# Self-attention with outputs of three of four key tiles moved to the following slot

## Chip, cores and metric

The kernel runs on one core of a Trainium2 chip. The metric is the device time of one execution in microseconds (us). Engines are named as the profile names them: PE is TensorE's matmul, PEld its weight load, DVE is VectorE, ACT is ScalarE, POOL is GpSimd, SP is SyncE. Each engine works through its own list of instructions in order, and waits for the others by semaphores.

## The reference

The input `x` is 8 batches of 512 rows of width 512 in float32. It passes through a cross-attention block with adaptive layer norm, and then through a diffusion transformer block: self-attention, cross-attention to a context of 77 rows per batch, and an MLP. Only self-attention bears on the change:

```python
x_norm = modulate(_ln(x), shift_a, scale_a)
qkv = x_norm @ W_qkv + b_qkv
q, k, v = jnp.split(qkv, 3, axis=-1)          # 16 heads of 32
...
attn_w = jax.nn.softmax(jnp.einsum('bhqd,bhkd->bhqk', q, k) * scale, axis=-1)
attn_out = jnp.einsum('bhqk,bhkd->bhqd', attn_w, v)
...
attn_out = attn_out @ W_proj + b_proj
x = x + gate_a[:, None] * attn_out
```

## The kernel before

The program has four phases, one after the other: cross-attention "x", self-attention "a", cross-attention "c", and the MLP. Self-attention is the function `self_phase`. In it the order of all instructions is the order of the Python statements, on every engine; nothing is rescheduled.

The work is cut into 32 groups: batch `b` (0 to 7) times `fc` (0 to 3), where one `fc` is four heads, 128 columns. A group has 512 keys, cut into four key tiles `k` of 128, and all 512 queries. Scores are held transposed, keys on the partitions and queries along the row. Two heads share a tile of 128 x 1024, so each key tile has two tiles `e`. The steps of a group, as methods of `Group`:

- `scores(k)`: eight matmuls (`sT_a`, L803) write two PSUM tiles. ACT copies each to `e` (L821); from k = 1 on DVE takes a running maximum over the key tiles into `mx_a` (L823). Both PSUM tiles of the pool are used by one score step, so the next one needs the copies and maxima done.
- `maxima()`: DVE transposes and reduces `mx_a` (L834, L835) to `part_a`, four times.
- `spread()`: PE transposes `part_a` (`mxT_ps_a`, L843), DVE reduces it and negates it (L847), SP writes it to DRAM as `mxd_a` (L852).
- `shift(k)`: POOL issues two DMAs (L857) that read `mxd_a`, the same row for all 128 partitions, and add it to the two `e` tiles of 512 KB. Per group that is eight DMAs, 4.19 MB.
- `exp(k)`: ACT, in place, two instructions (L866).
- `add_up(k)`: adds the two `e` tiles to the sum over key tiles, on POOL for k = 1 and 2, on DVE for k = 3 (L873).
- `outputs(k)`: eight matmuls (L886) accumulate `o_ps_a` over the key tiles.
- `total()`: eight matmuls with ones (L896) give the denominators `z_ps_a`.
- `finish()`: DVE takes the reciprocal (L903) and multiplies (L906) into `oT_a`.

The main loop has 31 passes; a pass is called a slot here. In a slot, group `g` is shifted, exponentiated and summed with V, while the scores of the next group `nxt` are made. In between stand TensorE's other tasks of the slot, given by `beside(b, fc)` as four pieces f[0] to f[3] of eight matmuls each: values, queries and keys of later groups, and the output projections of the batch before (`project`, L353, with the residual sum on DVE at L772, products and sums on POOL at L775 and L776 in `flush(0)`, stores on SP at L779 in `flush(1)`). In fc 2, `transpose_x` adds four groups of PE transposes (L724), and `load_x` loads the next batch's rows. In fc 0, `load_tile` loads four residual tiles `xr_a` (L718). `normalise_x` feeds layer norm pieces to DVE.

The `e` tiles come from two pools of eight, one for even and one for odd groups: group n + 1 takes the tiles of group n - 1. PSUM has four banks for scores, two for the pool `ps_m` that projections, values, queries, keys and transposes share, and two for `o_ps_a` and `z_ps_a`.

Of the kernel before, what the change touches and what calls it, by code (L numbers as in the profile page):

```python
# [10 lines left out]
F32 = mybir.dt.float32  # L11
# [7 lines left out]
P = 128  # L19
H = 512  # L20
# [59 lines left out]
def tile_pixart_block(ctx: ExitStack, tc: tile.TileContext, a: dict, out: bass.AP):  # L80
    nc = tc.nc
    x, ctx_in, cond = a["x"], a["ctx_1024"], a["cond_1024"]
    B, N, _ = x.shape
    S = ctx_in.shape[1]
    NT = N // P
# [272 lines left out]
    def run(gen):  # L358
        while True:
            try:  # L360
                next(gen)
            except StopIteration as stop:
                return stop.value
# [28 lines left out]
    def normalise_x(nm, b):  # L392

        xb = [x_sb[nm, 0][:, t, :] for t in range(NT)]
        mv, y = yield from ln_stats_pieces(xb, P, 1e-6, f"{nm}{b}")
        yield
        for t in range(NT):
            normalise(xb[t], xb[t], mv, y, t, P)
            if t % 2:
                yield  # L400


    with tc.tile_pool(name="ps_s", bufs=2, space=PSUM, reuse_waits="tile") as ps_s:
# [287 lines left out]
        def self_phase(w, bo_row, work, work_2, ctx_c):  # L691
# [14 lines left out]
            def flush(part):  # L706

                while later[part]:
                    later[part].popleft()()

            def load_x(b):
                nc.scalar.dma_start(
                    out=x_cur, in_=x_src["a"][b].rearrange("(t p) d -> p t d", p=P)
                )

            def load_tile(b, t, queue=nc.scalar):
                xr = work.tile([P, H], F32, tag="xr", bufs=4, name=f"xr_a{b}_{t}")
                queue.dma_start(out=xr, in_=x_src["a"][b][ts(t, P), :])  # L718
                st[b]["x"][t] = xr

            def transpose_x(b, k):
                pt = ps_m.tile([P, H], F32, tag="m", name=f"lnT_ps_a{b}_{k}")
                for t in range(NT):
                    nc.tensor.transpose(pt[:, ts(t, P)], x_cur[:, t, ts(k, P)], ident)  # L724
                o = work.tile([P, N], F32, tag="xnT", bufs=5, name=f"xnT_a{b}_{k}")
                nc.scalar.activation(  # L726
                    o, pt, AF.Identity,
                    bias=mod_l1[:, k, b : b + 1], scale=mod_l1[:, KC + k, b : b + 1],
                )
                st[b]["xT"].append(o)  # L730
# [54 lines left out]
            class Group:  # L785
# [91 lines left out]
                def outputs(self, k):  # L877

                    if k == 0:
                        self.po, self.pz = [  # L880
                            ps_o.tile([P, H], F32, tag="o", name=f"{nm}_ps_{self.nm}")
                            for nm in "oz"
                        ]
                    vt = st[self.b]["v"][k]
                    for h in range(4):
                        nc.tensor.matmul(  # L886
                            self.po[ts(h, HD), :],
                            lhsT=vt[:, self.fc * P + h * HD : self.fc * P + (h + 1) * HD],
                            rhs=self.e[k][h // 2][:, h % 2, :],
                            start=(k == 0), stop=(k == NT - 1),  # L890
                        )

                def total(self):

                    for h in range(4):
                        nc.tensor.matmul(  # L896
                            self.pz[ts(h, HD), :], lhsT=ones, rhs=self.sum[:, h, :],
                            start=True, stop=True,
                        )
# [28 lines left out]
            def pump(gen, n):  # L928
                for _ in range(n):
                    next(gen, None)  # L930
# [10 lines left out]
                first.scores(k)  # L941
                run(gen)
            first.maxima()
            first.spread()
            last, ln = None, normalise_x("a", 1)
            for n, g in enumerate(groups[:-1]):
                b, fc = g.b, g.fc
                nxt = groups[n + 1]
                more = b + 1 < B
                f = beside(b, fc)  # L950
                if fc == 3:
                    ln = normalise_x("a", b + 2) if b + 2 < B else iter(())
                if fc == 0 and b > 0:
                    for t in range(NT):
                        load_tile(b - 1, t)
                for k in range(NT):
                    g.shift(k)
                flush(0)
                flush(1)
                if not more and fc == 1:  # L960
                    ctx_c.w_k = load_w("L1_xcond_W_kvc", 0)
                nxt.scores(0)
                if last is not None:
                    last.total()
                    last.finish()
                pump(f[0], 4)
                if fc == 2 and more:
                    transpose_x(b + 1, 0)
                    transpose_x(b + 1, 1)
                nxt.scores(1)  # L970
                if fc != 2 and more or fc == 2 and not more:
                    next(ln, None)
                g.exp(0)
                pump(f[1], 4)
                if fc == 1 and not more:
                    ctx_c.load()
                    ln = ctx_c.norm()
                if fc == 2 and more:
                    transpose_x(b + 1, 2)
                    transpose_x(b + 1, 3)  # L980
                nxt.scores(2)
                if fc == 1 and more:
                    for _ in ln:
                        pass
                elif fc != 2 and more or fc == 2 and not more:
                    next(ln, None)
                g.exp(1)
                flush(0)
                g.add_up(1)
                pump(f[2], 3)  # L990
                nxt.scores(3)
                pump(f[2], 1)
                g.exp(2)
                g.add_up(2)
                g.outputs(0)
                g.outputs(1)
                nxt.maxima()
                pump(f[3], 4)
                g.outputs(2)
                nxt.spread()  # L1000
                if fc == 2 and not more:
                    next(ln, None)
                g.exp(3)
                g.add_up(3)
                if fc == 2 and not more:
                    for _ in ln:
                        pass
                if fc == 2 and b + 2 < B:
                    load_x(b + 2)
                g.outputs(3)  # L1010
                last = g

            g = groups[-1]
            for k in range(NT):
                g.shift(k)
            flush(0)
            flush(1)
            work_2.release()
            kv = tc.alloc_tile_pool(name="kv_c", bufs=1, side="right", reuse_waits="tile")
            ctx_c.room(kv)  # L1020
            last.total()
            last.finish()
            ctx_c.transpose()
            run(ctx_c.values(0))
            run(ctx_c.values(1))
            value = None
            for k in range(NT):
# [348 lines left out]
```

## Time and profile before

| | us |
|---|---|
| three runs | 2659.38, 2662.30, 2663.26; median 2662.3 |
| the profiled execution: its time | 2658.09 |
| the profiled execution: its span | 2656.3 |
| PE busy in the span | 2519.7 (95%) |
| DVE / ACT / POOL busy in the span | 1742.3 / 1062.3 / 830.2 |
| mean granted TensorE clock | 0.984 |
| self-attention's slots (first to last issue of `mxd_a`) | 527.66 to 1398.36 |

The profile is of one execution. A row of a timeline gives the start, the duration, the engine, the line, the operation and its tiles, and in brackets how long the engine had been idle and who released it. Busy time of PE says little here, as the ends of matmuls are modelled; distances between starts say more. Rows of POOL with DMA_DIRECT2D are the issue of a DMA; when its data has landed is given separately.

### The profile page before, as it was taken

Reading aid. Unit: us, or ns where it says so; the run is one execution under the profiler, and the core shown is the slowest. Engines: PE = TensorE matmul, PEld = TensorE weight load, DVE = VectorE, ACT = ScalarE, POOL = GpSimd, SP = SyncE. Lnnn points to the kernel's source line nnn. Section 1 sums busy time; section 2 is a strip of 40 time slices with the busy share of each in tenths; the row PEclk is TensorE's granted clock in tenths of the full one; section 3 lists DMA queues with packets and bytes.
Section 4 is the critical chain, followed back from the end, with each engine's and each line's share of the span. In section 5 each row is a group of like instructions: output and inputs, shape, how many; then the busy total and the mean of one; then the engine's idle time right before and its main releaser. Section 6 shows DMA issues by size and latency. Waiting matters only on the chain.

```text
span 2656.3 us, 32748 instructions
## 1 busy us (share of the span) xinstructions
PE 2519.7 (95%) x12517; PEld 1436.6 (54%) x12517; DVE 1742.3 (66%) x3131; ACT 1062.3 (40%) x1442; POOL 830.2 (31%) x692
## 2 busy tenths in 40 slices
PE   7999999889999999999988999999999999999998
PEld 3555554322323333332323555555788888888887
DVE  2676677377777777877674777776655555555553
ACT  1533333366666676665663443442211211211220
POOL 1000001156766767677574010112211011011011
PEclk9999999999999999999998999999999999999999
DMA  7011211189898898998898111114011111111010
GB/s 261 28 52 52 80 57 68 64 162 185 174 179 181 176 194 178 179 185 174 174 195 225 60 40 53 40 42 137 16 37 38 30 36 38 30 36 40 28 36 24
DMA packets 116407, 264.90 MB, mean 100 GB/s; under 512 B 12594, under 2 KB 29058, under 8 KB 116250
## 3 DMA queue, kind: packets, MB, share of 16 engines
q0 software_dynamic: 37152, 134.28, 26.9%
q1 hardware_dynamic: 69125, 109.42, 12.4%
q10 hardware_dynamic: 9973, 19.11, 2.2%
q8 instruction: 99, 1.62, 0.2%
q14 instruction: 58, 0.48, 0.1%
HBM read 226.39 MB, written 36.37 MB: 99 GB/s over the span
## 4 chain that ended last, share of the span: by engine, by line
PE 40%; issue 26%; DMA 15%; DVE 9%; POOL 6%; ACT 4%; POOLq 0%; SPq 0%; ACTq 0%; DVEq 0%
DMA e_a<-mxd_a 12%; PE proj_ps_c L353 4%; PE proj_ps_x L353 4%; PE q_ps_c L345 4%; PE q_ps_x L345 4%; PE proj_ps_a L353 3%; PE sT_a L803 2%; PE pT_ps_c L621 2%; PE pT_ps_x L621 2%; DVE tu_a L834 2%; DVE part_a L835 2%; POOL res_m L1285 2%; POOL xr L1286 2%; DVE mx_a L823 2%; PE v_ps L353 2%
## 5 line engine op out<-in xcount | busy, mean ns | idle before, releaser
L821 ACT COPY e_a<-sT_a 128x1024 f32<-128x1024 f32 x256 | 253.5, 1012 | 155.0 <-PE sT_a L803 112.5
L866 ACT ACTIVATE e_a<-e_a 128x1024 f32<-128x1024 f32 x256 | 263.1, 1056 | 60.0 <-DMA e_a<-mxd_a 59.6
L857 POOL DMA_DIRECT2D e_a<-mxd_a x256 | 228.1, 2061 | 132.2 <-DMA mxd_a<-mxT_a 114.1
L1285 POOL TENSOR_TENSOR res_m<-res_m,gate_m 128x256 f32<-128x256 f32 x64 | 52.1, 814 | 665.9 <-DVE res_m L1283 665.9
L823 DVE TENSOR_TENSOR mx_a<-sT_a,mx_a 128x1024 f32<-128x1024 f32 x128 | 154.1, 1220 | 85.4 <-PE sT_a L803 59.7
L873 POOL TENSOR_TENSOR sum_a<-e_a,e_a 128x1024 f32<-128x1024 f32 x64 | 151.1, 2381 | 168.2 <-ACT e_a L866 168.2
L1219 ACT ACTIVATE hT<-hT,bcol 128x512 f32<-128x512 f32 x128 | 91.9, 721 | 237.4 <-DVE hT L1194 229.3
L886 PE MATMUL o_ps_a<-e_a,v 128*32 128x512 f32 x1024 | 167.8, 622 | 17.7 <-ACT e_a L866 17.4
L803 PE MATMUL sT_a<-qT_a,kT_a 32*128 32x512 f32 x1024 | 156.4, 666 | 20.2 <-ACT e_a L821 19.4
L372 POOL TENSOR_TENSOR x_x<-x_x,res_x 128x512 f32<-128x512 f32 x32 | 40.6, 1269 | 413.7 <-DVE res_x L368 255.2
L873 POOL TENSOR_TENSOR sum_a<-sum_a,e_a 128x1024 f32<-128x1024 f32 x64 | 149.9, 2364 | 9.0 <-ACT e_a L866 8.9
L622 ACT COPY pT_x<-pT_ps_x 77x512 f32<-77x512 f32 x128 | 72.9, 578 | 191.3 <-PE pT_ps_x L621 191.2
L903 DVE RECIPROCAL rz_a<-z_ps_a 128x512 f32<-128x512 f32 x32 | 107.4, 3357 | 63.9 <-PE z_ps_a L896 63.9
L372 POOL TENSOR_TENSOR x_c<-x_c,res_c 128x512 f32<-128x512 f32 x32 | 40.6, 1270 | 344.3 <-DVE res_c L368 287.5
L622 ACT COPY pT_c<-pT_ps_c 77x512 f32<-77x512 f32 x128 | 72.8, 577 | 162.8 <-PE pT_ps_c L621 162.8
L345 PE MATMUL q_ps_x<-xnT_x,w_L_xcond_Wq 128*128 128x512 f32 x256 | 135.1, 614 | 0.0
L1186 PE MATMUL q_ps_h<-x_m,w_L_xcond_W_mlp 128*128 128x256 f32 x512 | 132.3, 381 | 0.0
L345 PE MATMUL q_ps_a<-xnT_a,w_L_xcond_W_qkv 128*128 128x512 f32 x256 | 130.9, 637 | 0.7 <-ACT xnT_a L726 0.7
L1186 PE MATMUL q_ps_h<-xT_m,w_L_xcond_W_mlp 128*128 128x256 f32 x512 | 131.4, 379 | 0.0
L345 PE MATMUL q_ps_c<-xnT_c,w_L_xcond_W_qc 128*128 128x512 f32 x256 | 130.1, 594 | 0.0
L1186 PE MATMUL q_ps_h<-x_m,w_s 128*128 128x256 f32 x512 | 122.2, 382 | 5.9 <-DVE w_s L1140 4.9
L353 PE MATMUL v_ps<-w_L_xcond_W_qkv,xnT_a 128*128 128x512 f32 x256 | 118.9, 607 | 0.0
(248 smaller groups left out, 5016.0 us busy)
## 6 DMA issues: line engine op xcount, KB each, us to landing
e_a<-mxd_a POOLq DMA_DIRECT2D x256, 512.0 KB, 13.9
xa<-x_x SPq DMA_DIRECT2D x32, 256.0 KB, 2.0
xc<-xr_a SPq DMA_DIRECT2D x32, 256.0 KB, 2.6
x_c<-xc SPq DMA_DIRECT2D x8, 1024.0 KB, 6.3
w_L_xcond_W_mlp<-in_L_xcond_W_mlp_dram SPq DMA_DIRECT2D x8, 1024.0 KB, 6.1
xm<-x_c SPq DMA_DIRECT2D x32, 256.0 KB, 2.0
x_m<-xm SPq DMA_DIRECT2D x8, 1024.0 KB, 5.2
xr<-xm SPq DMA_DIRECT2D x64, 128.0 KB, 3.6
```

The costliest lines, as they stand in the source:

```text
L345: nc.tensor.matmul(ps, lhsT=w[:, k, ts(j, P)], rhs=xT[k], start=(k == 0), stop=(k == KC - 1))
L353: nc.tensor.matmul(ps, lhsT=xT[k][:, cols], rhs=w[:, k, :], start=(k == 0), stop=(k == KC - 1))
L622: nc.scalar.copy(pTs[-1][:, h % 2, :], pp[:S, :])
L803: nc.tensor.matmul(sc[h // 2][:, h % 2, :], lhsT=kT[ts(h, HD), ts(k, P)], rhs=qT[ts(h, HD), :], start=True, stop=True,)
L821: nc.scalar.copy(self.e[k][i], sc[i])
L823: nc.vector.tensor_tensor(self.mx[1 - i], sc[1 - i], self.e[0][1 - i] if k == 1 else self.mx[1 - i], ALU.max,)
L857: nc.gpsimd.dma_start(out=self.e[k][i].rearrange("p h n -> p (h n)"), in_=self.mxd[2 * i : 2 * i + 2, :] .rearrange("h n -> (h n)").partit ...
L866: nc.scalar.activation(self.e[k][i], self.e[k][i], AF.Exp)
L873: engine.tensor_tensor(sum_i, self.e[0][i] if k == 1 else sum_i, self.e[k][i], ALU.add)
L886: nc.tensor.matmul(self.po[ts(h, HD), :], lhsT=vt[:, self.fc * P + h * HD : self.fc * P + (h + 1) * HD], rhs=self.e[k][h // 2][:, h % 2, : ...
L903: nc.vector.reciprocal(r, self.pz)
L1186: nc.tensor.matmul(self.banks[n][:, half], lhsT=lhsT, rhs=rhs, start=(k == 0), stop=(k == len(pairs) - 1),)
```

## The change

The loop is rearranged; no arithmetic is added or taken away.

- Outputs of key tiles 1, 2 and 3 of group `g`, its `add_up(2)`, `add_up(3)`, `exp(3)`, `total` and `finish` move to the slot after. There they stand behind the score step of `nxt` that precedes the one taking that tile's buffers: outputs 1 after scores 0, outputs 2 after scores 1, outputs 3 and the total after scores 2. The group before is called `prev`.
- `spread` of group `g` moves from the end of the slot before (between outputs 2 and 3) to the start of the slot of `g`, behind scores 0 and outputs 1.
- `add_up(2)` of `prev` stands ahead of the eight shifts on POOL.
- `o_ps_a` keeps the pool of two buffers for itself; `z_ps_a` is taken from `ps_m`.
- The third piece f[2] is cut 2 + 2 around scores 3, where it was 3 + 1. `finish` stands ahead of scores 3.
- The loads of `xr_a` go from ACT's queue to SP's, behind the write of `mxd_a` and the stores. `load_x` moves from the end of the fc 2 slot to its middle. The layer norm pieces stand behind the shifts.
- The end of the phase does the same with the last two groups.

```diff
                 def outputs(self, k):
                     if k == 0:
-                        self.po, self.pz = [
-                            ps_o.tile([P, H], F32, tag="o", name=f"{nm}_ps_{self.nm}")
-                            for nm in "oz"
-                        ]
+                        self.po = ps_o.tile([P, H], F32, tag="o", name=f"o_ps_{self.nm}")
...
                 def total(self):
+                    self.pz = ps_m.tile([P, H], F32, tag="m", name=f"z_ps_{self.nm}")
...
             first.maxima()
-            first.spread()
-            last, ln = None, normalise_x("a", 1)
+            prev, ln = None, normalise_x("a", 1)
...
-                if fc == 0 and b > 0:
-                    for t in range(NT):
-                        load_tile(b - 1, t)
-                for k in range(NT):
-                    g.shift(k)
-                flush(0)
-                flush(1)
...
                 nxt.scores(0)
-                if last is not None:
-                    last.total()
-                    last.finish()
+                if prev is not None:
+                    prev.outputs(1)
+                g.spread()
+                if prev is not None:
+                    prev.add_up(2)
+                    prev.exp(3)
+                for k in range(NT):
+                    g.shift(k)
+                flush(1)
+                if fc == 0 and b > 0:
+                    for t in range(NT):
+                        load_tile(b - 1, t, nc.sync)
...
                 pump(f[0], 4)
...
                 nxt.scores(1)
-                g.exp(0)
+                if prev is not None:
+                    prev.outputs(2)
+                    prev.add_up(3)
                 pump(f[1], 4)
+                flush(0)
...
                 if fc == 2 and more:
                     transpose_x(b + 1, 2)
                     transpose_x(b + 1, 3)
+                    if b + 2 < B:
+                        load_x(b + 2)
                 nxt.scores(2)
-                g.exp(1)
-                flush(0)
-                g.add_up(1)
-                pump(f[2], 3)
-                nxt.scores(3)
-                pump(f[2], 1)
-                g.exp(2)
-                g.add_up(2)
-                g.outputs(0)
-                g.outputs(1)
-                nxt.maxima()
-                pump(f[3], 4)
-                g.outputs(2)
-                nxt.spread()
-                g.exp(3)
-                g.add_up(3)
-                if fc == 2 and b + 2 < B:
-                    load_x(b + 2)
-                g.outputs(3)
-                last = g
+                if prev is not None:
+                    prev.outputs(3)
+                    prev.total()
+                g.exp(0)
+                pump(f[2], 2)
+                if prev is not None:
+                    prev.finish()
+                nxt.scores(3)
+                pump(f[2], 2)
+                g.exp(1)
+                g.add_up(1)
+                nxt.maxima()
+                g.outputs(0)
+                pump(f[3], 4)
+                flush(0)
+                g.exp(2)
+                prev = g
```

The lines that place the layer norm pieces, and the end of the phase, are left out of this diff.

More of the change, by code (lines that the diff above doesn't have):

```diff
@@ L962, in self_phase @@
                 nxt.scores(0)
-                if last is not None:
-                    last.total()
-                    last.finish()
+                if prev is not None:
[10 more added lines that the diff above has]
+                        load_tile(b - 1, t, nc.sync)
+                if fc in (0, 3) and more:
+                    next(ln, None)
+                    if fc == 3 or b == 0:
+                        next(ln, None)
+                elif fc == 1 and more:
+                    for _ in ln:
+                        pass
+                elif fc == 2 and not more:
+                    next(ln)
+                    next(ln)
                 pump(f[0], 4)
@@ L970, in self_phase @@
                 nxt.scores(1)
-                if fc != 2 and more or fc == 2 and not more:
-                    next(ln, None)
-                g.exp(0)
+                if fc == 2 and not more:
+                    next(ln)
+                if prev is not None:
+                    prev.outputs(2)
+                    prev.add_up(3)
                 pump(f[1], 4)
+                flush(0)
                 if fc == 1 and not more:
@@ L980, in self_phase @@
                     transpose_x(b + 1, 3)
+                    if b + 2 < B:
+                        load_x(b + 2)
                 nxt.scores(2)
[L982 to L986, printed above, removed]
+                if prev is not None:
[7 more added lines that the diff above has]
+                pump(f[2], 2)
                 g.exp(1)
+                g.add_up(1)
+                nxt.maxima()
+                g.outputs(0)
+                pump(f[3], 4)
                 flush(0)
-                g.add_up(1)
-                pump(f[2], 3)
-                nxt.scores(3)
-                pump(f[2], 1)
                 g.exp(2)
-                g.add_up(2)
-                g.outputs(0)
-                g.outputs(1)
-                nxt.maxima()
-                pump(f[3], 4)
-                g.outputs(2)
-                nxt.spread()
-                if fc == 2 and not more:
-                    next(ln, None)
-                g.exp(3)
-                g.add_up(3)
-                if fc == 2 and not more:
-                    for _ in ln:
-                        pass
-                if fc == 2 and b + 2 < B:
-                    load_x(b + 2)
-                g.outputs(3)
-                last = g
+                prev = g
             g = groups[-1]
+            prev.outputs(1)
+            g.spread()
+            prev.add_up(2)
             for k in range(NT):
                 g.shift(k)
-            flush(0)
             flush(1)
+            run(ln)
+            ctx_c.transpose()
+            prev.exp(3)
+            prev.outputs(2)
+            prev.add_up(3)
+            run(ctx_c.values(0))
+            prev.outputs(3)
+            prev.total()
+            prev.finish()
             work_2.release()
@@ L1020, in self_phase @@
             ctx_c.room(kv)
[L1021 to L1024, printed above, removed]
             run(ctx_c.values(1))
```

## The prediction

> **What bounds the kernel now.** The page comes first. Its row of DMA shares and its chain of waits put the trouble in one stage.
>
> ```profile
> DMA  7011211189898898998898111114011111111010
> PE 40%; issue 26%; DMA 15%; DVE 9%; POOL 6%; ACT 4%; POOLq 0%; SPq 0%; ACTq 0%; DVEq 0%
> ```
>
> Slices 9 to 21 (about 530 to 1400 us) are self-attention: the 16 DMA engines stand at 80 to 99% there and near 10% elsewhere, and 12 of the chain's 15% of DMA are the transfers `e_a<-mxd_a`. Second view: SP's timeline. `mxd_a` is written once per slot (one pass of the loop), so the distances of its issues are slot lengths: 527.66, 638.77, 1310.91 and 1398.36 us bound batch 0 (111.1 us, four slots), batches 1 to 6 (672.1 us, 24 slots, 28.0 each) and three slots of batch 7 (87.5). By kind, from 917.48 on: fc 2 29.9, fc 3 27.5, fc 0 27.0, fc 1 27.0 us. Third: TensorE's timeline of that last one.
>
> ```profile
> 1001.15 0.30 PE L843 MATMUL mxT_ps_a<-ident,part_a 128*64 128x128 f32 x1 [1.07 <-DVE part_a L835]
> 1001.38 1.05 PE L886 MATMUL o_ps_a<-e_a,v 128*32 128x512 f32 x4
> 1003.41 1.05 PE L886 MATMUL o_ps_a<-e_a,v 128*32 128x512 f32 x4 [0.97 <-ACT e_a L866]
> 1004.39 1.14 PE L803 MATMUL sT_a<-qT_a,kT_a 32*128 32x512 f32 x8
> ...
> 1028.20 0.30 PE L843 MATMUL mxT_ps_a<-ident,part_a 128*64 128x128 f32 x1 [0.90 <-DVE part_a L835]
> ```
>
> Columns: start, duration, what, and in brackets the idle time before and who ended it. Starts differ by 0.23 us for the small transpose, 1.07 for a score step, 1.00 for an output step or a total, 3.63 for a projection: 0.23 + 4 x 1.07 + 4 x 1.00 + 1.00 + 4 x 3.63 = 24.0 us of work in 27.05. The rest is about 1 us at `mxT` and 1.5 us inside the last output step. That output step waits for exp, exp for the DMA. POOL and the DMA queue, same slot:
>
> ```profile
> 1004.00 7.12 POOL L857 DMA_DIRECT2D e_a<-mxd_a  x8 [2.49 <-DMA mxd_a<-mxT_a]
> ```
>
> The DMA view of 1004 to 1029 us: the rate in 40 slices, and the shifts' median from issue to landing.
>
> ```profile
> GB/s 164 111 98 177 210 210 184 170 177 138 111 138 170 210 210 216 203 216 210 210 210 210 210 210 210 210 223 210 197 223 210 210 223 203 210 197 105 13 0 0
> e_a<-mxd_a POOLq DMA_DIRECT2D x8, 512.0 KB, 12.9
> ```
>
> The eight shifts leave 2.85 us after `mxT` starts (call that start S) and run one after another: by the tile's view the first lands 4.9 us after its issue, and the last exp starts at 1028.30, S + 24.3. So shift number j lands at S + 4.9 + 2.77 j. The last columns (25 us in 40) show the queue empty until the next S. **The loop**: `mxT`, S after 2.85, landing after 24.3, exp, output: 27 us, longer than 24.0 of work. In fc 2, four groups of transposes (0.59 each) make the work 24.0 + 4 x 0.59 = 26.4, and waits for evacuation add to it. TensorE's waits over 23 of these slots:
>
> ```profile
> PE mxT_ps_a L843 <- DVE part_a L835: 25.8, 24, 1.6
> PE o_ps_a L886 <- ACT e_a L866: 8.6, 12, 1.2
> PE sT_a L803 <- ACT e_a L821: 6.9, 5, 2.1
> PE lnT_ps_a L724 <- ACT xnT_a L726: 5.2, 6, 0.9
> ```
>
> Only 1.1 us a slot is for the maxima; the rest of the 3.4 us (28.0 less the mean work of 24.6) is late exp, in part hidden in weight loads, and slow matmuls after it.
>
> **The Trainium skill.** "Perfetto Trace Analysis", DMA Instruction (SWDGE): POOL's window ends when the descriptors are written, not when data has moved. The trace agrees: 7.1 us on POOL for eight, 24 us to the last landing. "DMA: Bandwidth & Descriptors", Issuing engines are not separate DMA queues: a load moved from ACT to SP saves issue time alone, and still shares the 16 engines. Here ACT stood 18.4 us in 6 slots behind the issue of `xr_a`, and those 256 KB loads land in 4.7 us. "TensorE: Matmul & The Clock Gate", What's actually happening: an idle window of about 3.4 us halves the clock. The trace agrees: after 4.21 us idle at 564.68 a score step took 2.16 us, not 1.14.
>
> **The change, part by part.** No arithmetic is added or removed; order and buffers change. Times count from the start of `mxT` in a slot.
>
> Outputs 1, 2, 3, the total and `finish` move one slot later; 4 x 1.00 us still lie on TensorE once per slot. What goes is the wait of the last output for the landing: exp(3) may be as late as the next slot. What is late next is DVE. `finish` (reciprocal and product, 4.00 us: 1006.62 to 1010.62) moves to stand between the maxima of score steps 2 and 3. Loop of a slot: `mxT` 0.23, project 3.63, scores 1.07, outputs 1.00, project 3.63: score step 2 starts at 9.56. From its start DVE needs 3.70 (1018.63 to 1022.33), then 4.00, 2.30 for score step 3's maxima and 5.82 for the transposed maxima (1022.33 to 1028.15), 0.05 to the next `mxT`: 15.87. Sum **25.4 us**, 1.4 of it TensorE's wait, against 27.0 to 28.5 before.
>
> `spread` moves from between outputs 2 and 3 to behind score step 0 and outputs 1 of the next slot: one TensorE transpose, one DVE reduction (0.28), one SP issue (0.45). It waited for the maxima before and does so still, with 2.07 us of other TensorE work ahead of it. The normalising pieces on DVE now follow it (four statistics with their aggregates 3.4 us, or twelve small ones 2.0, or four products 2.2): they end 3.9 after `mxT`, the maxima of score step 1 start at 5.1. `add_up(3)`, 2.4 us on DVE, stands between the maxima of steps 1 and 2: from 7.6 to 10.0, and the residual's 0.68 after it ends at 10.7, when step 2's maxima may begin (10.8). Hidden, but without slack: if exp(3) is late by t, the loop grows by t.
>
> `z_ps` in the pool of `q`, `k` and projections: of two buffers it holds one until the reciprocal ends, 7.7 after score step 2; the key projection that takes it comes at 8.8. Hidden; without that cover at most the 3.4 us reciprocal is added, below nothing is excluded since it only adds a wait. Two `o` buffers replace o and z: no wait.
>
> POOL: `add_up(2)`, 4.7 us, is now ahead of the shifts. exp(1) ends at 21.3 and 22.3; two add-ups of 4.7 bring POOL to 30.8, that is 5.4 in the next slot, so S moves from 2.85 to 5.4. POOL's residual products (2 x 2.54) stand behind the shifts' 7.1 and end before exp(1). Landings: exp(0) 13.1 (ACT free at 13.2), exp(1) 18.5 (20.3), exp(2) 24.1 (23.0: waits 1.1), exp(3) 29.6, 4.2 in the next slot. Behind exp(2) on ACT queue the copies of score step 0 (done at 2.7); score step 1 needs them at 3.86: 1.1 us of margin. exp(3) is done by 5.3 to 6; step 1's copies then end at 8, step 2 needs them at 9.56. All hidden, with 1 to 1.5 us to spare. I add 0.4 us a slot for what this misses; the bounds are 0 and 1.5.
>
> SP: four `xr` loads (1 MB) move from ACT to SP, behind `mxd_a` and the stores. ACT's 3 us per fc 0 go, but the loads now meet the tail of the last shifts: up to 4 us later landing of exp(3), 1.4 us past the margin. So fc 0 is 26.8. `load_x` (1 MB, one issue of 0.38 on ACT) moves to the middle of fc 2 and delays shifts by up to 5 us; fc 2 is longer by 3, which absorbs it. Stores and the gate load fall into POOL's wait. Fc 2: 25.4 + 2.4 of transposes + 0.9 of evacuation waits (two of 0.35 to 0.5) = 28.7.
>
> Sum. Batches 1 to 6: 26.8 + 25.8 + 28.7 + 25.8 = 107.1 against 112.0 measured, -29.5. Batch 0 has few projections and waits most for exp on ACT; my estimate from the same rows is 22 to 26 a slot, 99 for 111.1, -12. Batch 7: fc 1 carries 2.2 MB of weights and context, stays near 29; the two others give -5.5. The tail keeps its work and waits less, -2. Together **-49 us**: 2658.1 (profiled execution; its span 2656.3 and 1.8 around it) becomes 2609. The median of the runs shown stands 4.2 above the profiled one: 2613.
>
> **Rivals.**
> *All cover holds* (chance 0.11): TensorE is the bound, 24.6 a slot: 24 x 3.4 + 14 + 9 = -105, 2557; halfway there 2582. Against it: DVE's loop of 25.4 holds unless the maxima shrink.
> *The DMA queue is the bound* (0.08). Its share over 665 to 1311 us is 0.89 of 28.0 = 25.0 us a slot. At the 0.95 of the best whole slot that is 26.3, below my mean of 26.8; only if it can't rise over 0.89 does nothing change, 2662. Against: shares of 1.04 to 1.08 over 1006 to 1020 us.
> *Late landings through ACT's queue* (0.13; slower). exp(2) stands ahead of the copies of score step 0, and those hold score step 1. The loop S, exp(2), copies, step 1, step 2, step 3, exp(1), two add-ups, S spans two slots in 49.7 us. It decides when landings are over 1.1 us late, and equals the old 28.0 a slot when they are 6.3 us late; at 8 us a slot is 28.9: 28 x 0.9 = +25, 2687. For: S is itself 2.5 us later, and loads share the engines. Against: the queue had emptied before each S.
> *It doesn't do what it says*: the order of the changed program's instructions shows outputs 1 to 3 after score steps 0 to 2 on TensorE, and the add-up ahead of the shifts. Excluded.
>
> **The numbers.** Likeliest, 0.68: 2613, from 2590 (no 0.4, batch 0 -15) to 2646 (1.5 us missed in each slot). Range 2588 to 2648: it leaves out half of the first rival and most of the third. A measurement tells 0.2% (5 us) from no change. Faster 0.82 (0.68 + 0.11 + 0.03 of the DMA case), same 0.05, slower 0.13.
>
> **What would show it.** SP's `mxd_a` issues 25 to 27 us apart, fc 2 at 28 to 29; no wait of `o_ps` for exp in TensorE's list; the wait of `mxT` for `part_a` grown to about 1.4 us; S about 5.4 us after `mxT`, right behind `add_up(2)`; DMA share in the stage 0.93 or more. A list led by `sT_a` waiting for ACT's copies, or slots over 28, would make it wrong.

## The result and the profile after

The changed kernel takes 2635.4 us (median of four runs, 2632.2 to 2638.6) against 2661.8 us for the kernel before (four runs, 2659.4 to 2663.3): a ratio of 0.990, 95% interval 0.9885 to 0.9919. It is faster, and 2635 lies inside the range, but the gain is 26 us where 49 were forecast. The profiled execution took 2635.31 us, its span is 2633.5, so by the spans of the two profiles the gain is 22.8 us.

Outputs are now L883, the total L894, `finish` L901 and L904; the other lines of the steps keep their numbers. First the page, its row of DMA shares over 40 slices, and its chain of waits.

```profile
DMA  7011212289898998999988111113011011011010
...
issue 24%; PE 16%; POOL 5%; DMA 1%; DVE 1%; ACT 0%; POOLq 0%; SPq 0%; ACTq 0%
```

The DMA row hardly differs: a queue that stands at 80 to 99% before and after can't tell whether anybody waits for it. The chain can't tell it either this time. Its shares add up to 47%: it starts at 1375 us, behind self-attention, so its 1% of DMA says nothing about the stage. What tells it is TensorE's own list of waits in the stage (650 to 1290 us: who waited, for what, us in total, times, longest):

```profile
PE sT_a L803 <- ACT kT_a L758: 24.5, 24, 1.6
PE lnT_ps_a L724 <- DVE res_a L772: 15.5, 12, 2.2
PE mxT_ps_a L843 <- DVE part_a L835: 8.3, 19, 0.6
PE z_ps_a L894 <- DVE sum_a L873: 2.0, 4, 0.9
```

The wait of `o_ps_a` for exp is gone, as the prediction said. Three waits grew or are new: score step 0 for ScalarE's copy of the keys, the transposes of fc 2 for the residual on VectorE, and the total for the sum. The first is the longest of the list, but behind it `mxT` still waits for VectorE in 19 of 24 slots, so time saved at score step 0 would be spent waiting at `mxT` (see e3); the second is the one that matters. The start of POOL's shifts is where it was forecast, 5.3 us after `mxT` (982.75), right behind `add_up(2)`, by POOL's timeline:

```profile
983.21 4.86 POOL L873 TENSOR_TENSOR sum_a<-sum_a,e_a 128x1024 f32<-128x1024 f32 x2
988.01 7.16 POOL L857 DMA_DIRECT2D e_a<-mxd_a  x8
```

One batch as stages, slot by slot from fc 0 to fc 3 (window; its length; busy us of PE, PEld, DVE, ACT, POOL with instructions; granted clock, DMA share, GB/s):

```profile
957.57:983.40 25.83, 24.29 (x107) 7.96 (x106) 24.82 (x32) 18.88 (x23) 16.44 (x13) 1.00 1.02 211
983.40:1011.40 28.00, 25.40 (x107) 7.93 (x106) 27.30 (x25) 16.71 (x19) 22.20 (x17) 1.00 0.89 172
1011.40:1042.48 31.08, 27.72 (x123) 9.99 (x122) 22.17 (x22) 19.80 (x23) 22.12 (x17) 0.95 0.87 186
1042.48:1067.47 24.99, 24.01 (x107) 7.84 (x106) 22.03 (x28) 18.11 (x22) 16.21 (x13) 1.00 0.88 174
```

The two long slots, fc 1 and fc 2, are the ones with the lowest DMA share beside fc 3's and with the busiest POOL. In fc 1 VectorE is busy 27.3 of 28.0 us; in fc 2 TensorE's clock sags to 0.95. The table gives slot lengths by kind as means over batches 1 to 6 (between successive reductions of `mxT_ps_a` on VectorE, the first instruction after `mxT`), for all kernels of this document. In the changed kernel fc 1 is 28.0 to 28.4 us in four of these batches and 26.5 in two, and fc 2 is 31.1 in five and 29.75 in one, so a few tenths in these means say nothing. The last column is the median of the runs; each experiment ran beside the kernel before on the same chip (medians 2662.6 to 2663.3 there), and its ratio is to those runs.

| kernel | fc 0 | fc 1 | fc 2 | fc 3 | six batches | whole |
|---|---|---|---|---|---|---|
| before | 27.77 | 26.45 | 30.09 | 27.71 | 672.1 | 2661.8 |
| predicted | 26.8 | 25.8 | 28.7 | 25.8 | 642.6 | 2613 |
| after | 25.84 | 27.57 | 30.89 | 24.99 | 655.8 | 2635.4 |
| e7: after, two of eight shifts left out | 25.91 | 28.02 | 30.69 | 25.00 | 657.7 | 2634.1 |
| e8: before, the same two left out | 27.05 | 26.09 | 29.08 | 28.02 | 661.4 | 2647.1 |
| e4: loads put back | 25.94 | 27.69 | 30.71 | 25.25 | 657.6 | 2645.9 |
| e3: outputs 0 behind the keys | 25.84 | 27.78 | 30.42 | 25.00 | 654.2 | 2634.2 |
| e1: normalisation left out | 25.84 | 26.43 | 30.84 | 25.00 | 648.7 | 2625.7 |
| e12: residual products left out | 25.86 | 26.62 | 27.91 | 25.06 | 632.7 | 2609.3 |
| e13: residual ahead of `add_up(3)` in fc 2 | 25.85 | 28.00 | 29.39 | 25.00 | 649.4 | 2630.5 |
| e2: residual products later | 25.93 | 26.60 | 30.19 | 28.50 | 667.3 | 2655.2 |
| e9: `add_up(2)` behind the shifts | 31.72 | 33.38 | 32.93 | 32.18 | 781.2 | 2786.9 |
| e5: `add_up(2)` on VectorE | 25.00 | 25.00 | 29.76 | 25.43 | 631.2 | 2611.2 |
| e10: e5, transposes spread | 25.00 | 25.00 | 27.84 | 27.05 | 629.4 | 2608.8 |
| e11: e10, load and statistics later | 25.12 | 28.13 | 27.56 | 25.00 | 634.8 | 2608.2 |

Where the missing 26.2 us are (49 less 22.8, by profiles), each term measured minus predicted: six batches 13.1, batch 0 5.6 (104.7 us instead of 99.1), three slots of batch 7 5.3 (87.2 instead of 82), what lies before and after 2.2. Within the six batches fc 0 and fc 3 are better than forecast by 1.8 us together, fc 1 and fc 2 worse by 4.0.

**The theory.** VectorE and POOL hold each other up when both work on SBUF, which the durations taken from the profile before hardly contained. The profile's view of groups on VectorE in 650 to 1290 us, before and after (a group, its instructions | busy us, mean ns of one | idle before). Before:

```profile
L873 DVE TENSOR_TENSOR sum_a<-sum_a,e_a 128x1024 f32<-128x1024 f32 x46 | 54.8, 1212 | 3.5 <-ACT e_a L866 3.5
...
L301 DVE TENSOR_SCALAR x_a<-x_a,mv_a,lny_a 128x512 f32<-128x512 f32 x24 | 15.0, 665 | 0.0
...
L288 DVE TENSOR_SCALAR lnv_a<-mv_a 128x4 f32<-128x4 f32 x6 | 1.0, 159 | 0.0
```

After:

```profile
L873 DVE TENSOR_TENSOR sum_a<-sum_a,e_a 128x1024 f32<-128x1024 f32 x46 | 70.6, 1575 | 0.0
...
L301 DVE TENSOR_SCALAR x_a<-x_a,mv_a,lny_a 128x512 f32<-128x512 f32 x24 | 36.0, 1560 | 0.0
...
L288 DVE TENSOR_SCALAR lnv_a<-mv_a 128x4 f32<-128x4 f32 x5 | 11.4, 2285 | 0.0
```

The same instructions on the same shapes: an operation on four numbers per partition goes from 0.16 to 2.29 us, the normalising product from 0.67 to 1.56 (0.53 in e5, so that the profile before held a little of it), `add_up(3)` from 1.21 to 1.58 on average. VectorE's timeline shows the neighbours, two from fc 0 and fc 1 beside `add_up(2)`, two of `add_up(3)`, in fc 2 and fc 3:

```profile
957.47 2.28 DVE L288 TENSOR_SCALAR lnv_a<-mv_a 128x4 f32<-128x4 f32 x1
...
983.29 6.07 DVE L301 TENSOR_SCALAR x_a<-x_a,mv_a,lny_a 128x512 f32<-128x512 f32 x4
...
1019.51 4.13 DVE L873 TENSOR_TENSOR sum_a<-sum_a,e_a 128x1024 f32<-128x1024 f32 x2
...
1049.07 2.35 DVE L873 TENSOR_TENSOR sum_a<-sum_a,e_a 128x1024 f32<-128x1024 f32 x2
```

Of the four L301 the first two take 2.56 and 2.58 us, about the length of one of POOL's two additions beside them (983.21 and the next, 2.35 and 2.54), and the last two, with POOL at its shifts, 0.54. `add_up(3)` has its two instructions at 1.21 in fc 3, where POOL only issues shifts, and takes 4.13 in fc 2, where POOL's residual product (L775) begins at 1020.16. The changed kernel has its own control: in batches 3 and 5 L775 begins 0.5 to 0.8 us later in fc 1, with the second instruction of `add_up(3)`, which then takes 2.34 instead of 3.71 or more. These are the two slots fc 1 of 26.5 us. VectorE's and POOL's timelines in batch 3:

```profile
883.53 2.34 DVE L873 TENSOR_TENSOR sum_a<-sum_a,e_a 128x1024 f32<-128x1024 f32 x2
...
884.69 3.69 POOL L775 TENSOR_TENSOR res_a<-res_a,gate_a 128x512 f32<-128x512 f32 x1
```

The Trainium skill describes this, and the prediction didn't use it: "SBUF — State Buffer", Who interferes with whom, says that VectorE and GpSimd share one pair of ports, that `tensor_scalar` can take both of VectorE's port pairs if its operands allow it, in which case whoever comes second waits for the other's whole instruction, and that a VectorE instruction with two SBUF inputs contends with GpSimd's reads. The trace agrees, with the numbers above: `tensor_scalar` took as long as POOL's addition. Also as the page says, an instruction with one SBUF input that does not take both pairs isn't touched: the maxima's transposes (L834) stay at 0.71 beside POOL's `add_up(1)`. That the ports are the reason is the page's account; the runs below show only that POOL's work at that place makes VectorE's instructions longer.

Rivals: **D**, late landings of the shifts and the loads that meet them set the long slots; **K**, score step 0's wait for the copy of the keys lengthens every slot.

### The profile page after: what moved, and what is told of

Same layout as the page of the kernel before. It is cut to its first block, busy times and chain, and to the rows that moved or that the text cites. A ratio compares the mean times of both kernels' runs of the same rounds, so it can differ in the third digit from the quotient of the medians.

```text
span 2633.5 us, 32580 instructions
## 1 busy us (share of the span) xinstructions
PE 2494.5 (95%) x12517; PEld 1430.5 (54%) x12517; DVE 1802.4 (68%) x3131; ACT 1060.3 (40%) x1442; POOL 834.0 (32%) x692
## 3 DMA queue, kind: packets, MB, share of 16 engines
q0 software_dynamic: 37152, 134.28, 27.3%
## 5 line engine op out<-in xcount | busy, mean ns | idle before, releaser
L883 PE MATMUL o_ps_a<-e_a,v 128*32 128x512 f32 x1024 | 146.3, 630 | 4.7 <-ACT e_a L866 4.7
L353 PE MATMUL proj_ps_a<-w_L_xcond_W_proj,oT_a 128*128 128x512 f32 x256 | 119.6, 611 | 0.0
L353 PE MATMUL proj_ps_c<-w_L_xcond_W_cproj,oT_c 128*128 128x512 f32 x256 | 118.3, 604 | 0.5 <-DVE oT_c L633 0.5
```

What stands on the lines that cost most here:

```text
L353: nc.tensor.matmul(ps, lhsT=xT[k][:, cols], rhs=w[:, k, :], start=(k == 0), stop=(k == KC - 1))
L883: nc.tensor.matmul(self.po[ts(h, HD), :], lhsT=vt[:, self.fc * P + h * HD : self.fc * P + (h + 1) * HD], rhs=self.e[k][h // 2][:, h % 2, : ...
```

## The experiments

**e7 and e8, two of eight transfers left out.** One edit, in the changed kernel and in the kernel before:

```diff
-                for k in range(NT):
+                for k in range(NT - 1):
                     g.shift(k)
```

> The changed kernel without the shifts of key tile 3 (its scores are not lowered by the maxima; 2 of 8 transfers per slot left out). Theory: landings no longer bound anything, no slot changes by more than 0.5 us except that POOL is 1.8 us less busy; whole 2628 to 2637. Rival D: fc 1 and fc 2 shorter by 1.5 or more, whole under 2615.

> The kernel before without the shifts of key tile 3, the same two transfers of eight left out. Theory (the last landing, exp and output closed the loop of before): the last landing comes 5.5 us earlier, the loop falls to what the maxima and TensorE allow, 25 to 26 us and 28.5 to 29.5 in fc 2, 26.0 to 26.7 on average against 28.0; whole 2625 to 2640. If landings were not the bound of before: 2655 to 2665.

e7: 2634.1 us, no different from the changed kernel. With a quarter of the traffic gone, fc 1 and fc 2 stay at 28.0 and 30.7. So neither the queue nor the last two landings bound the changed kernel. Six of the eight transfers remain in e7. That the changed kernel doesn't wait for these either is read from its trace: in the lists of waits of TensorE and VectorE (650 to 1290 us) no entry is for exp or for ScalarE's copies of the scores. By both, and by e4 for the loads, D is out. e8: 2647.1, ratio to before 0.9937 (0.9921 to 0.9954). Landings did bound the kernel before, but the last one isn't all of it: 10.7 us in six batches came where 31 to 48 were expected, and the whole missed the expected 2625 to 2640. TensorE's list of e8 in 650 to 1290 us shows which part went:

```profile
PE mxT_ps_a L843 <- DVE part_a L835: 25.5, 21, 1.9
PE sT_a L803 <- ACT e_a L821: 8.9, 9, 1.9
...
PE o_ps_a L886 <- ACT e_a L866: 0.9, 2, 0.5
```

The outputs' wait for exp fell from 8.6 to 0.9, the scores' wait for ScalarE's copies rose from 6.9 to 8.9. ScalarE's and TensorE's timelines in a slot fc 3 of e8 show what that is:

```profile
955.17 1.06 ACT L866 ACTIVATE e_a<-e_a 128x1024 f32<-128x1024 f32 x1 [2.31 <-DMA e_a<-mxd_a]
...
956.60 1.93 ACT L821 COPY e_a<-sT_a 128x1024 f32<-128x1024 f32 x2
```

```profile
958.58 1.47 PE L803 MATMUL sT_a<-qT_a,kT_a 32*128 32x512 f32 x8 [1.64 <-ACT e_a L821]
```

exp(0) waits for the second transfer, the copies of score step 2 stand behind it in ScalarE's queue, and score step 3 waits for those. So in this slot one of the first landings also stood in the way. The change moves exp(0) behind score step 2 and exp(1) behind step 3, which the prediction described only as an effect on the last output. That this move brought the rest is read from the trace; it was not tried alone.

**e4, the loads put back.**

```diff
-                        load_tile(b - 1, t, nc.sync)
+                        load_tile(b - 1, t)
...
-                    if b + 2 < B:
-                        load_x(b + 2)
                 nxt.scores(2)
...
                 g.exp(2)
+                if fc == 2 and b + 2 < B:
+                    load_x(b + 2)
```

> Undoes one part of the change: the residual's four loads in fc 0 are issued by ScalarE again and the next x is loaded at the end of fc 2 again. Theory (VectorE against POOL): fc 2 stays within 0.5 us of 30.9 and fc 1 within 0.5 of 27.6; ScalarE's 3 us of issuing in fc 0 cost 0 to 2 us there; whole 2632 to 2647. Rival D (loads that meet the shifts lengthen fc 2 and fc 1): fc 2 falls by 1.0 or more, whole under 2628.

2645.9 us, slower than the changed kernel by 10, with fc 2 at 30.7 and fc 1 at 27.7. The moved loads don't lengthen the long slots. Of the 10 us only 1.8 are in the six batches; 2.7 are in batch 0 and 4.0 in batch 7 (91.2 us for its three slots, 87.2 in the changed kernel). The other 2.1 us by profiles lie outside self-attention's slots. So some 10 of the change's 26 us hang on the place of these loads, most of it at the ends of the phase; by what way, these traces don't settle.

**e3, outputs 0 behind the key projection.**

```diff
-                g.outputs(0)
                 pump(f[3], 4)
+                g.outputs(0)
```

> Moves output step 0 (1.0 us of TensorE) behind the key projection, so that it covers ScalarE's copy of the keys, for which score step 0 waits 0.8 to 1.6 us in nearly every slot. Theory: VectorE's chain sets fc 0, fc 1 and fc 3, so there the wait only moves to the transpose of the maxima; fc 2 alone gets shorter, by 0.5 to 1.0; whole 2628 to 2633. Rival K: every slot loses 0.8 to 1.0, whole 2607 to 2613.

2634.2 us, no change (2628 to 2633 were expected). The edit took away little of the wait of score step 0 for the keys: 21.0 us are left of 24.5. But `mxT`'s wait rises from 8.3 to 13.9, and now `mxT` waits for VectorE in all 24 slots: what is left of the keys' wait is covered there, and what was taken away comes back there. Fc 2, where `mxT` did not wait before, gains 0.5. So the trace speaks against K more than the time does; the longest wait in the list was hardly a cost.

**e1, the normalising products left out.**

```diff
         for t in range(NT):
-            normalise(xb[t], xb[t], mv, y, t, P)
+            if scaled:        # False in self-attention
+                normalise(xb[t], xb[t], mv, y, t, P)
```

> Leaves out the four products that normalise x in self-attention (they stand at the head of slot fc 1 on VectorE, 6.07 us in the changed kernel where 2.2 were assumed); its output is then that of an x that is not normalised. Theory (VectorE and POOL slow each other down when both work on SBUF): fc 1 falls from 27.6 us on average to 25.5 to 26.5, fc 0, 2 and 3 stay at 25.8, 30.9 and 25.0; the whole at 2622 to 2629 us against 2635. Rival D (late landings of the shifts set the long slots): fc 1 stays at 27 to 28, whole 2633 to 2637.

2625.7 us; fc 1 is 26.43, the others don't move: within the expectation. In fc 1 these four products cost 1.1 us of the slot, net: the edit takes out their work together with its slowing. In batch 3 of e1 `add_up(3)` also stays at 1.22 us for each instruction, and there fc 1 is 25.00. That fc 0 stays at exactly 25.84 fits too, as its slowed small operations are still there.

**e12, the residual products left out on POOL**, and **e13, the residual ahead of `add_up(3)` in fc 2.** fc 2's long wait is seen in TensorE's timeline of the changed kernel:

```profile
1021.53 0.60 PE L724 MATMUL lnT_ps_a<-ident,x_a 128*128 128x128 f32 x4
1024.30 0.66 PE L724 MATMUL lnT_ps_a<-ident,x_a 128*128 128x128 f32 x4 [2.16 <-DVE res_a L772]
1024.88 2.09 PE L803 MATMUL sT_a<-qT_a,kT_a 32*128 32x512 f32 x8
1026.91 1.70 PE L883 MATMUL o_ps_a<-e_a,v 128*32 128x512 f32 x8
```

The fourth transposes need the buffer of the second projection, which the residual sum (L772) has to read first; that sum stands on VectorE behind `add_up(3)`, which took 4.13 us. Behind the gap the score step and the outputs run at a reduced clock, 2.09 and 1.70 us instead of 1.14 and 1.07. Five of the six slots fc 2 have such a stretch; the one without it, in batch 2, is 1.3 to 1.4 us shorter (columns as in the table of stages above, batches 2 and 4):

```profile
793.99:823.74 29.75, 26.20 (x122) 9.69 (x121) 22.04 (x21) 19.90 (x22) 21.98 (x17) 1.00 0.89 191
1011.09:1042.17 31.08, 27.72 (x122) 9.99 (x121) 22.14 (x22) 19.63 (x22) 22.12 (x18) 0.95 0.87 186
```

The two edits take away the supposed cause, and the supposed way in which it acts:

```diff
# e12
                         def add():
-                            nc.gpsimd.tensor_tensor(tmp, tmp, st[b]["g"], ALU.mult)
-                            nc.gpsimd.tensor_tensor(xr, xr, tmp, ALU.add)
+                            pass
# e13
                     prev.outputs(2)
-                    prev.add_up(3)
+                    if fc != 2:
+                        prev.add_up(3)
                 pump(f[1], 4)
+                if prev is not None and fc == 2:
+                    prev.add_up(3)
```

> Leaves out POOL's products and sums of the residual (gate times projection plus x, in all batches), so x leaves self-attention as it came; no other instruction of POOL moves. Theory (VectorE's add_up(3) is slowed to 3.7 and 4.1 us by these products, the residual queues behind it, and the transposes of fc 2 wait for the residual): add_up(3) takes 2.35 us in every slot, the transposes' waits for the residual fall from 15.5 us in six batches to about 5, fc 2 falls from 30.9 to 28.5 to 29.4 us, fc 1 by 0.5 to 1.4; the whole, with 5 to 8 us saved at the end of batch 7 too, at 2604 to 2622. Rival (fc 2 is long because of its own transposes and their two buffers, whatever the products do): add_up(3) gets shorter but fc 2 stays at 30.3 or more.

> In fc 2 alone, add_up(3) stands behind the second residual sum on VectorE instead of ahead of it, so the transposes' buffer comes free however slow add_up(3) is; nothing else moves. Theory: the transposes' waits of about 2.2 us become 0.4, the clock stays full, fc 2 falls from 30.9 to 28.5 to 29.5, fc 1 stays at 27.6; the whole at 2619 to 2628. Rival (fc 2 is held by something that comes after, such as the sum that total() needs): fc 2 stays at 30.3 or more, with a new wait of z_ps_a for sum_a of 1 us or more.

e12: 2609.3 us, as expected; fc 2 is 27.91, below the expected 28.5, and fc 1 26.62. e13: 2630.5; fc 2 is 29.39, and its whole time misses the expected 2619 to 2628 because batch 7's fc 2 grew to 36.3 us from 32.9. TensorE's wait of the transposes in 650 to 1290 us, e12 first, then e13:

```profile
PE lnT_ps_a L724 <- DVE res_a L772: 4.4, 12, 0.4
```

```profile
PE lnT_ps_a L724 <- DVE res_a L772: 5.0, 12, 0.4
PE z_ps_a L894 <- DVE sum_a L873: 2.2, 6, 0.4
```

Both bring the 15.5 us to 4.4 or 5.0. In e12 the 48 instructions of `add_up(3)` take 1.21 to 1.22 us each, so the products were what slowed it; e13 leaves them slow (up to 2.58) and still gains 1.5 us in fc 2, as the residual no longer stands behind them. So fc 2's 3.0 us (30.89 to 27.91) are POOL's products, about half of it by way of the residual and the transposes. Most of that half is the clock: e13's six slots fc 2 are all 29.39 at a granted clock of 1.00, only 0.36 below the changed kernel's slot at full clock. The rival of e13, the total's sum, takes 0.4 us a slot.

**e2, the residual products behind `add_up(1)`.**

```diff
                 pump(f[1], 4)
-                flush(0)
...
                 g.add_up(1)
+                flush(0)
                 nxt.maxima()
```

> Moves POOL's products of the residual (gate times projection, plus x) from the middle of the slot to behind add_up(1), so that they no longer stand beside add_up(3) on VectorE. Theory: add_up(3) takes 2.35 us again in fc 1 and fc 2 (3.7 and 4.1 before), the second transposes of fc 2 no longer wait 2.2 us for the residual, fc 2 falls from 30.9 to 28.5 to 29.5 and fc 1 by 0.5 to 1.3; the whole at 2613 to 2625. POOL's own add-up may now come later by the products' 5 us in fc 2 and 1, so up to 3 us of that may be given back. Rival D (landings): fc 2 stays at 30.5 or more, 2633 or above. Rival K (the wait of score step 0 for the copy of the keys is what lengthens the slots): no change, 2635.

2655.2 us, slower by 20: a miss. fc 3 grew by 3.5 us. POOL's and VectorE's timelines in its slot fc 2 (`mxT` at 1018.44):

```profile
1024.03 4.69 POOL L873 TENSOR_TENSOR sum_a<-sum_a,e_a 128x1024 f32<-128x1024 f32 x2
1028.65 7.11 POOL L857 DMA_DIRECT2D e_a<-mxd_a  x8
```

```profile
1027.19 3.75 DVE L873 TENSOR_TENSOR sum_a<-sum_a,e_a 128x1024 f32<-128x1024 f32 x2
```

The products push `add_up(2)` 5 us back, and now that is what stands beside `add_up(3)`: 3.75 us. The shifts leave 10.2 us after `mxT`, and by the trace this is what lengthens fc 3. In the slot fc 3 that follows (from 1049.18) ScalarE's exp waits for the shifts, its copies of the scores stand behind exp, and VectorE waits for the copies. VectorE's list of waits in 650 to 1290 us has an entry for it, which the changed kernel's list doesn't have (15.9 of the 16.7 us are in slots fc 3):

```profile
DVE mx_a L823 <- ACT e_a L821: 16.7, 11, 3.1
```

This is the prediction's rival of late landings through ScalarE's queue: at 5.3 us after `mxT` the shifts cost nothing, at 10.2 us they do. POOL has work for this stretch of the slot whatever the order; moving it only changes what meets what.

**e9, `add_up(2)` behind the shifts.**

```diff
                 if prev is not None:
-                    prev.add_up(2)
                     prev.exp(3)
                 for k in range(NT):
                     g.shift(k)
+                if prev is not None:
+                    prev.add_up(2)
```

> Undoes one part of the change: POOL issues the shifts first and does add_up(2) behind them. The shifts leave 2.5 us earlier, nothing of POOL's stands beside VectorE's small operations at the slot's head. Theory: add_up(3) on VectorE adds to the same sum and has to wait for add_up(2), which ends at 3 + 7.1 + 4.7 = 14.8 us of the slot; the maxima of step 2 queue behind it, the loop becomes 14.8 + 2.35 + 2.35 + 4.0 + 2.3 + 5.8 = 31.6 us, whole 2740 to 2790. Rival D (landings set the long slots): under 2625.

2786.9 us (ratio to before 1.047), fc 0 at 31.7: as worked out. VectorE's timeline:

```profile
985.72 5.57 DVE L873 TENSOR_TENSOR sum_a<-sum_a,e_a 128x1024 f32<-128x1024 f32 x2 [4.17 <-POOL sum_a L873]
```

The later shifts (5.3 us after `mxT`) are the price of having the sum in time, and nothing in the changed kernel's lists waits for them.

**e5, `add_up(2)` on VectorE**, behind the normalising pieces at the head of the slot:

```diff
-                    engine = nc.vector if k == NT - 1 else nc.gpsimd
+                    engine = nc.vector if k >= NT - 2 else nc.gpsimd
...
                 if prev is not None:
-                    prev.add_up(2)
                     prev.exp(3)
...
+                if prev is not None:
+                    prev.add_up(2)
                 pump(f[0], 4)
```

> Takes add_up(2) off POOL and does it on VectorE, at the head of the next slot behind the small normalising operations. POOL then has only the shifts' issue there, which starts about 3 us after mxT instead of 5.3. Theory: the four products of fc 1 take 2.2 us again (6.07), the tiny operations of fc 0 0.16 each (two of them 2.28); VectorE gains 2.35 us of work per slot, in the idle 3 to 5 us at the head of the slot; fc 1 falls to 26 to 27, fc 2 stays near 31, whole 2620 to 2632. Rival D (landings set the long slots): landings 2.4 us earlier, fc 1 and fc 2 both fall by 2 or more, whole under 2612. Rival V (VectorE is full by its own work): every slot grows by up to 2.35, whole up to 2700.

2611.2 us, ratio to before 0.9808 (0.9793 to 0.9823): better than the theory's own figure. VectorE's groups in 650 to 1290 us:

```profile
L301 DVE TENSOR_SCALAR x_a<-x_a,mv_a,lny_a 128x512 f32<-128x512 f32 x24 | 11.4, 531 | 0.0
...
L288 DVE TENSOR_SCALAR lnv_a<-mv_a 128x4 f32<-128x4 f32 x5 | 0.8, 151 | 0.0
```

VectorE does 2.35 us more per slot and the slots get shorter. fc 0 and fc 1 both sit at 25.00 us. That this is just under D's 2612 does not speak for D: fc 2, which D said would fall by 2, fell by 1.1, and the changed kernel's lists show no wait for landings (e7). The edit does bring the landings forward too, so the split between the two rests on those lists.

**e10, e5 and the transposes spread**, and **e11, e10 with load and statistics later.**

```diff
# e10, on e5
                     transpose_x(b + 1, 0)
-                    transpose_x(b + 1, 1)
                 nxt.scores(1)
+                if fc == 2 and more:
+                    transpose_x(b + 1, 1)
...
                     transpose_x(b + 1, 2)
-                    transpose_x(b + 1, 3)
-                    if b + 2 < B:
-                        load_x(b + 2)
                 nxt.scores(2)
+                if fc == 2 and more:
+                    transpose_x(b + 1, 3)
+                    if b + 2 < B:
+                        load_x(b + 2)
# e11, on e10: load_x behind g.exp(2) at the end of fc 2, and
-                if fc in (0, 3) and more:
+                if fc == 0 and more:
                     next(ln, None)
-                    if fc == 3 or b == 0:
-                        next(ln, None)
+                    next(ln, None)
```

> add_up(2) on VectorE at the head of the slot as in the run that did this alone (2611 us), and of the transposes of fc 2 the second and the fourth moved behind the score steps 1 and 2 that followed them, so that score steps cover the wait for the two buffers of q, k, projections and transposes. Theory: the waits of the transposes for the residual (0.35 and 1.06 us in one slot, 12.7 us in six batches) go and the clock stays full; fc 2 falls from 29.8 to 27.5 to 28.3, the others stay at 25.0 to 25.4; whole 2597 to 2603. If fc 2 is long for another reason (loads, landings): 2608 or more.

> As the run with add_up(2) on VectorE and the transposes spread (2608.8 us; fc 3 27.05 us there), but the next x is loaded at the end of fc 2 again, and its statistics move from the head of fc 3 to the head of fc 0, the small rsqrt operations from fc 0 to fc 1. Theory (in fc 3 the load now meets the last shifts: VectorE's statistics wait 2.4 us for it and ScalarE's exp(3), ahead of the copies of the scores, 1.5 us): fc 3 falls to 25.0 to 25.6, fc 0 and fc 1 rise by up to 1.0 since their heads hold 5.8 and 6.2 us of VectorE work; whole 2598 to 2608. If the load only moves its damage to the next slot: 2608 or more.

e10: 2608.8 us, ratio to before 0.9792 (0.9772 to 0.9811). fc 2 fell to 27.84 as expected, but fc 3 rose from 25.43 to 27.05, and the whole missed the expected 2597 to 2603. In a slot fc 3 of e10, VectorE's and ScalarE's timelines:

```profile
923.18 0.69 DVE L276 BATCH_NORM_STATS2 st_a<-x_a 128x6 f32<-128x512 f32 x1 [2.40 <-DMA x_a<-xa]
```

```profile
924.80 1.06 ACT L866 ACTIVATE e_a<-e_a 128x1024 f32<-128x1024 f32 x1 [1.48 <-DMA e_a<-mxd_a]
```

The shorter fc 2 no longer covers the 1 MB load: here late landings do bind. e11 takes that away (fc 3 is 25.00) and pays in fc 1, 28.13 where 26 at most was expected, where VectorE ran from `mxT` to `mxT` without a gap in one slot (969.46 to 997.32); 2608.2 us, which is at the border of the two expectations. The damage moved, but it is VectorE's work that does it in fc 1, not the load. e5, e10 and e11 all beat both kernels; e10 and e11 can't be told apart.

## Why the prediction was right in sign and off in size

- **The wait that goes.** Right in kind: outputs no longer wait for exp. That the last landing closed the old loop was only part of the truth (e8: 10.7 us of the 31 or more expected); by the trace of e8, exp(0) ahead of the copies in ScalarE's queue was another.
- **The loop of 25.4 us, VectorE's chain in TensorE's order.** Right: fc 3 is 24.99, and with no POOL addition at the slot's head fc 0 and fc 1 are 25.00 (e5). The allowance of 0.4 was not needed there.
- **"They end 3.9 after `mxT`", the normalising pieces.** This step failed. 2.0 and 2.2 us were taken from a profile in which POOL's additions stood elsewhere. Beside `add_up(2)`, which the same change puts there, the four products took 6.07, and two small operations 2.28 each. It is worth up to 1.1 us in fc 1 (e1), and the 0.84 by which fc 0 exceeds 25.00.
- **"Hidden, but without slack", `add_up(3)` and the residual.** This step failed too, for the same reason: 3.7 and 4.1 us instead of 2.4 in fc 1 and fc 2, 1.0 and 3.0 us of slot (e12).
- **Fc 2: 25.4 + 2.4 + 0.9 = 28.7.** Without the contention it is 27.91 (e12), so the sum itself was high; the 30.89 is contention. Within it the prediction left out the clock: it named an idle window of about 3.4 us, but a wait of 2.16 us was already followed by matmuls at a reduced clock, about 1.1 us of fc 2 on average (five of six slots, 1.4 us each).
- **Fc 0: 26.8, by late landing behind the `xr` loads.** Wrong in cause and size: 25.84, and what is over 25.00 is the small operations. ScalarE's 3 us of issuing in fc 0 were not worth a slot's time either: fc 0 is 25.94 with the loads put back (e4).
- **POOL and the shifts, S at 5.4.** Right (5.3), and at that time the landings were hidden (e7 and the lists of waits).
- **The signs.** Several of those that the prediction gave went against it. Fc 2 is at 30.9, not 28 to 29. `mxT`'s wait did not grow to 1.4 us a slot, it fell to 0.35 (8.3 in 24 slots). The DMA share of 0.93 or more did not appear: 0.89, 0.87 and 0.88 in three of the four slots shown. Both signs of being wrong came: slots over 28 us, and a list led by `sT_a` waiting for a copy of ScalarE's, though that of the keys, a wait that the prediction doesn't name.
- **The rivals.** The DMA queue as the bound is excluded for this kernel (e7). Late landings through ScalarE's queue left no wait in its lists, but the mechanism is real, and e2 shows it. "All cover holds" would need VectorE's loop shorter than 25.0, which no slot mean of batches 1 to 6 was in any run.
- **Batches 0 and 7.** 5.6 and 5.3 us were missed there. In batch 7 the products are part of it (fc 2 is 30.0 in e12, 32.9 in the changed kernel); in batch 0 the normalising products are 1.4 (e1). The remainder is open.

The contention terms, added as if they were independent, are per batch 1.1 + 1.0 in fc 1, 3.0 in fc 2 and 0.8 in fc 0: 5.9 us, 35 in six batches. That is more than the 13.1 that was missing there; the forecast was otherwise too cautious by the difference. So there was luck in the number: two errors stood against each other, and 2635 lies in the range because it allowed up to 1.5 us a slot for what was missed, not because contention was among the rivals.

## What to carry to other kernels

Before moving work in time, list what runs on POOL beside its new place: here a `tensor_scalar` of VectorE in SBUF took the length of POOL's instruction, whatever its own size, and an addition of two SBUF tiles up to two and a half times its own, so a duration from the old place is no estimate for the new one. The later transfers, which one would suspect first, had some microseconds to spare. In a tight loop, an addition may be cheaper on the busier VectorE than on the idler POOL, since on POOL it also slows its neighbours. The longest wait in a list need not be the cost: ask whether removing it moves the next synchronisation point.

## What the runs showed of the hardware that was not expected

- Two `tensor_scalar` operations on 128 x 4 took 2.28 us each on VectorE beside POOL additions of 128 x 1024 (2.36 us each), 0.15 to 0.17 us without them: the wait is as long as POOL's instruction, not as the operation.
- POOL's product L775 that begins while its shifts are still being issued is recorded with 4.59 us, later ones of the same shape with 1.27; `add_up(3)` on VectorE beside the long one took 3.0 us for one of its instructions, 1.21 beside shifts alone. Why it is recorded longer stays open; with six shifts instead of eight (e7) it is 3.46.
- TensorE's granted clock was 0.55 from 1024.8 to 1028.6 us, behind a wait of 2.16 us; in e13, where the same wait is at most 0.4, it is 1.00 in all six slots fc 2.
